# A graph layer's gather: one tile in five chunks fetched row by row by SyncE

## The chip, the cores and the metric

The kernel runs on one core of a Trainium2 chip. The metric is the device time of one execution in microseconds. A core has five engines with an instruction stream each: TensorE multiplies matrices (a weight load, then a matmul [...]), VectorE works element by element, ScalarE applies functions and copies, GpSimd is programmable and here only issues indirect gathers, and SyncE computes nothing and issues plain transfers. Transfers are carried out by 16 DMA engines [...]. Engines wait for each other and for transfers through semaphores.

## What is computed

Two relational graph layers on 50,000 nodes of 128 floats with 850,000 edges, then a residual layer norm. Cut to what matters:

```python
W   = einsum('rb,bio->rio', w_comp, basis)          # 16 relations from 8 bases
seg = dst * 16 + rel
agg = segment_sum(h[src], seg, 50000 * 16)          # sum the source rows by (target, relation)
msg = einsum('nri,rio->no', agg.reshape(N, 16, -1), W)
h   = relu(msg + h @ loop_w + bias)                 # twice: x -> H1 -> h
out = layernorm(x + h)
```

Edges come sorted by target node. The costly part is `h[src]`: 850,000 rows of 512 bytes, at random places in HBM, once for each layer.

## The kernel before

**Tiles and chunks.** 128 consecutive edges are a tile (6,641 tiles), ten tiles are a chunk (`K` = 10, so `C` = 665 chunks; the last one is short). Since the edges are sorted, the targets of a tile are few: a window of `WN` = 12 nodes from the tile's base node on. A chunk's tiles fall into one window of 128 nodes that starts at the chunk's base, `base_i[c]`.

**Preparation** (lines 151 to 293) loads the edges, turns them so that each tile's 128 source indices stand in one column of `src` and its slot numbers (relation and place in the window) in one column of `key`, computes the bases, and checks that all edges fit their windows (`good`). If they do, `chunked` runs (line 316), otherwise a slow general path, `summed`, which this input doesn't take.

**One chunk of one layer** (lines 379 to 419):

- `at(c)` loads the chunk's base node into a register of SyncE. SyncE loads the window's own 128 rows, `hw`, for the self loop, and in layer 2 also `xw` for the residual.
- Ten gathers (line 390, the helper is line 296): GpSimd issues one indirect transfer for each tile, 128 rows of 512 bytes, into `g[:, k, :]`. `g` has six buffers, so GpSimd may run up to six chunks ahead of TensorE.
- VectorE writes `hot` (line 392), a one-hot matrix of 192 slots (16 relations x 12 nodes) for every edge.
- TensorE multiplies each tile's rows by its one-hot matrix into `pa` (line 403), two tiles to a bank, three banks; ScalarE copies the bank to `aT` (line 410).
- After the second pair of tiles comes `finish` for the chunk before (line 415): `slots` sums over the relations (16 products with `W`, line 335); `nodes_of` moves the slots to nodes (`own`, line 347) and adds what the chunk before left over (`kept`, `shift`, line 351); the self loop is a transpose of `hw` (line 141), a copy to `hT` by ScalarE (line 143) and a product with `LOOP` (line 355); `ended` applies the relu and stores the window to `H1` from `h`, or in layer 2 adds the residual, normalises (`normed`: `st`, `mv`, `sd`, `rs`, `nm`, `o`) and stores to `out`. SyncE issues both stores.

**The order.** Each engine works through its instructions in order. The order is not that of the source: the framework's scheduler places instructions by its own costs, for instance the transpose of `hw` and two matmuls of the next tiles between the products with `W` and those with `own`, and the weight sums of the second layer (`combine(1)`, line 130, on VectorE), which are written at the end of the first layer, among the first chunks. The framework also gives every transfer one of its own semaphores in turn and puts the waits in.

**The layers.** Layer 2 gathers from `H1`, so its first gather waits for layer 1's last store.

Of the kernel before, what the change touches and what calls it, by code (L numbers as in the profile page):

```python
# [23 lines left out]
F32 = mybir.dt.float32  # L27
I32 = mybir.dt.int32
BF16 = mybir.dt.bfloat16
U8 = mybir.dt.uint8  # L30
AF = mybir.ActivationFunctionType
OP = mybir.AluOpType
# [4 lines left out]
P = 128  # L37
# [3 lines left out]
K = P // WN  # L41
S = K * WN
G = P // K * K
BATCH = 8
EPS = 1e-5
BANK = 512

# [6 lines left out]
def tile_rgcn_resnorm(  # L54
# [15 lines left out]
    nc = tc.nc  # L70
    N, D = x.shape
# [3 lines left out]
    C = -(-n_tiles // K)  # L75
# [6 lines left out]
    H1 = dram.tile([N, D], F32, name="H1")  # L82

    consts = ctx.enter_context(tc.tile_pool(name="consts", bufs=1))
# [16 lines left out]
    eps = consts.tile([P, 1], F32, name="eps")  # L101
    nc.vector.memset(eps, EPS)

# [42 lines left out]
    def column(j, first, ap):  # L146

        return bass.AP(tensor=edges.tensor, offset=edges.offset + j * E + first, ap=ap)
# [3 lines left out]
    src = consts.tile([P, n_groups * G], I32, name="src")  # L152
    key = consts.tile([P, n_groups * G], F32, name="key")

    base_i = consts.tile([1, C], I32, name="base_i")
    dist = consts.tile([P, C], F32, name="dist")
    slot = consts.tile([P, C], F32, name="slot")
    good = consts.tile([1, 1], I32, name="good")
    with tc.tile_pool(name="meta1", bufs=1) as m1, tc.tile_pool(name="meta", bufs=2) as mp:
# [14 lines left out]
        base1 = m1.tile([1, C], F32, name="base1")  # L174
        nc.vector.tensor_scalar(base1, tile_base[0:1], float(N - P), None, op0=OP.min)
        nc.vector.memset(base1[:, 0:1], 0.0)
        nc.vector.memset(base1[:, C - 1 :], float(N - P))
        nc.vector.tensor_copy(base_i, base1)

        spread = m1.tile([K, S], F32, name="spread")  # L180
        nc.gpsimd.iota(
# [12 lines left out]
        for c0 in range(0, C, D):  # L194
            cs = slice(c0, min(c0 + D, C))
            k = cs.stop - c0
# [7 lines left out]
            )  # L204
        nc.vector.memset(dist[:, C - 1 :], 0.0)
        nc.vector.tensor_tensor(dist[:, : C - 1], base[:, 1:], base[:, : C - 1], op=OP.subtract)
        n_batches = -(-n_groups // BATCH)
        picked = m1.tile([P, n_batches + 2], F32, name="picked")
        nc.vector.memset(picked, 0.0)
# [7 lines left out]
            op0=OP.is_le,  # L217
# [10 lines left out]
            op0=OP.is_lt,  # L228
# [3 lines left out]
        for i in range(n_batches):  # L232
            g0 = i * BATCH
            q = min(BATCH, n_groups - g0)
            t0 = g0 * G
# [7 lines left out]
            if whole < q:  # L243
# [29 lines left out]
                op0=OP.is_lt,  # L273
# [8 lines left out]
            for of, to, engine in ((srcf, src, nc.scalar.copy), (rel0, key, nc.vector.tensor_copy)):  # L282
                for h0 in range(0, q, BANK // P):
                    h = min(BANK // P, q - h0)
# [15 lines left out]
    def normed(t, m, sb):  # L300

        st = sb.tile([P, 6], F32, name="st")
        nc.vector.bn_stats(st[:m], t)
        mv = sb.tile([P, 2], F32, name="mv")
        nc.vector.bn_aggr(mv[:m], st[:m])
        sd = sb.tile([P, 1], F32, name="sd")
        nc.scalar.activation(sd[:m], mv[:m, 1:2], AF.Sqrt, bias=eps[:m])
        rs = sb.tile([P, 1], F32, name="rs")
        nc.vector.reciprocal(rs[:m], sd[:m])
        nm = sb.tile([P, 1], F32, name="nm")  # L310
        nc.vector.scalar_tensor_tensor(nm[:m], mv[:m, 0:1], -1.0, rs[:m], op0=OP.mult, op1=OP.mult)
        o = sb.tile([P, D], F32, name="o")
        nc.scalar.activation(o[:m], t, AF.Identity, bias=nm[:m], scale=rs[:m])
        return o

    def chunked():
        combine(0)
        with tc.tile_pool(name="gp", bufs=6) as gp, tc.tile_pool(name="hp", bufs=2) as hp, tc.tile_pool(
            name="sb", bufs=3
        ) as sb:  # L320

            def at(c):
                return nc.values_load(
                    base_i[0:1, c : c + 1],
                    engines=[mybir.EngineType.SP],
                    min_val=0,
                    max_val=N - P,
                    skip_runtime_bounds_check_because="bases are clamped to N - P, and no node is below 0",
                )

            def slots(c, k, aT, n):

# [28 lines left out]
            def ended(n, a, n0, xw):  # L361
                if n == 0:
                    h = sb.tile([P, D], F32, name="h")
                    nc.scalar.activation(h, a, AF.Relu)
                    nc.sync.dma_start(H1[ds(n0, P), :], h)
                else:
                    t = sb.tile([P, D], F32, name="t")
                    nc.vector.scalar_tensor_tensor(t, a, 0.0, xw, op0=OP.max, op1=OP.add)
                    nc.sync.dma_start(out[ds(n0, P), :], normed(t, P, sb))

            for n, of in enumerate((x, H1)):
                kept, late = None, None

                def finish(kept, c, k, aT, hw, n0, xw):
                    kept, a = nodes_of(c, k, slots(c, k, aT, n), kept, hw, n)
                    ended(n, a, n0, xw)
                    return kept

                for c in range(C):
                    ks = min(K, n_tiles - c * K)  # L380
                    n0 = at(c)
                    hw = sb.tile([P, D], F32, name="hw")
                    nc.sync.dma_start(hw, of[ds(n0, P), :])
                    xw = None
                    if n:
                        xw = sb.tile([P, D], F32, name="xw")
                        nc.sync.dma_start(xw, x[ds(n0, P), :])
                    g = gp.tile([P, K, D], F32, name="g")
                    for k in range(ks):
                        gather(g[:, k, :], of, src[:, c * K + k : c * K + k + 1])  # L390
                    hot = hp.tile([P, K, NR * WN], F32, name="hot")
                    nc.vector.tensor_tensor(  # L392
                        hot[:, :ks],
                        grid[:, None, :].to_broadcast([P, ks, NR * WN]),
                        key[:, c * K : c * K + ks, None].to_broadcast([P, ks, NR * WN]),
                        op=OP.is_equal,
                    )
                    aT = hp.tile([P, NR, S], F32, name="aT")
                    for k in range(0, ks, 2):
                        m = min(2, ks - k)  # L400
                        pa = ps_a.tile([P, BANK], F32, name="pa")
                        for i in range(m):
                            nc.tensor.matmul(  # L403
                                pa[:, i * NR * WN : (i + 1) * NR * WN],
                                g[:, k + i, :],
                                hot[:, k + i, :],
                                start=True,
                                stop=True,
                            )
                        nc.scalar.copy(  # L410
                            aT[:, :, k * WN : (k + m) * WN].rearrange("p r (i w) -> p i r w", w=WN),
                            pa[:, : m * NR * WN].rearrange("p (i r w) -> p i r w", i=m, w=WN),
                        )
                        if k == 2 and late is not None:
                            kept = finish(kept, *late)
                            late = None
                    if late is not None:
                        kept = finish(kept, *late)
                    late = c, ks, aT, hw, n0, xw
                finish(kept, *late)  # L420
                if n == 0:
                    combine(1)

# [188 lines left out]
```

## Time and profile before

| | |
|---|---|
| timed executions | 22,033.58 us, median of 3 (22,026.26 to 22,033.65) |
| profiled execution | span 16,729.1 us |
| TensorE | busy 13,415.4 us (80%) |
| its weight loads | 11,315.1 us (68%) |
| VectorE | 5,048.0 us (30%) |
| ScalarE | 4,657.3 us (28%) |
| GpSimd | 12,558.5 us (75%), 13,290 instructions |
| granted TensorE clock | 0.890 |
| DMA | 67 GB/s on average; GpSimd's queue (q0) 425,024 packets, SyncE's (q1) 505,723 |

The first row is the metric; the others come from one profiled execution, whose span is shorter than the timed executions. The page doesn't tell why. In the page's slices of the span all engines' shares are even over both layers. A matmul's share overstates how hard TensorE works, since matmuls overlap and their ends are modelled. Issue time of SyncE and ScalarE is not counted as busy; it stands in the timeline under "SPq" and "ACTq".

### The profile page before, as it was taken

What the parts mean: (1) busy time and instruction counts of PE and PEld (TensorE: products, weight loads), DVE (VectorE), ACT (ScalarE), POOL (GpSimd) and SP (SyncE); (2) the same over time, 40 slices, a digit from 0 to 9 for tenths busy, and PEclk for the clock granted to TensorE, in tenths of its full rate; (3) what the DMA queues carried; (4) which work ended last, traced back from release to release, by engine and by line L of the source; (5) the groups of instructions that cost most, each with busy time, mean ns of one, the idle gap of its engine ahead of it and who ended that gap; (6) DMA issues with size and microseconds to landing.
All of it is one profiled execution on the core that took longest, in us unless ns stands there. A gap on an engine that the chain in (4) does not pass through costs nothing.

```text
span 16729.1 us, 222138 instructions
## 1 busy us (share of the span) xinstructions
PE 13415.4 (80%) x78570; PEld 11315.1 (68%) x78570; DVE 5048.0 (30%) x10325; ACT 4657.3 (28%) x12650; POOL 12558.5 (75%) x13290
## 2 busy tenths in 40 slices
PE   6888888878888888888888888888878888888787
PEld 5666666666666666666666666666666666666666
DVE  4222222222222222222233333333333333333333
ACT  2222222222222222222223222222222222222222
POOL 6777777777777777777777777777777777777777
PEclk9888888888888888888888889898888888888888
DMA  3222222222222222222222222222222222222222
GB/s 75 64 64 64 64 64 64 64 64 64 64 64 64 64 64 64 64 64 64 64 66 69 69 69 69 69 69 69 69 69 69 69 69 69 69 69 69 69 69 66
DMA packets 934787, 1115.38 MB, mean 67 GB/s; under 512 B 272843, under 2 KB 721179, under 8 KB 933691
## 3 DMA queue, kind: packets, MB, share of 16 engines
q0 software_dynamic: 425024, 871.30, 18.4%
q1 hardware_dynamic: 505723, 228.35, 4.9%
q8 instruction: 649, 10.63, 0.3%
q14 instruction: 447, 3.66, 0.1%
q10 hardware_dynamic: 2944, 1.44, 0.0%
HBM read 1012.86 MB, written 87.16 MB: 66 GB/s over the span
## 4 chain that ended last, share of the span: by engine, by line
POOL 41%; PE 26%; DMA 17%; issue 16%; DVE 0%; POOLq 0%; ACT 0%; SPq 0%; DVEq 0%; ACTq 0%
POOL g L296 41%; PE ps L335 16%; DMA g<-H,src 8%; DMA g<-in_x_dram,src 8%; PE pa L403 6%; PE pn L347 1%; PE pn L351 1%; PE po L355 1%; PE po L141 0%; DMA raw<-in_edges_dram 0%; DMA first_i<-in_edges_dram 0%; POOLq L296 0%; PE pa L287 0%; DVE rel L263 0%; DVE rel L277 0%
## 5 line engine op out<-in xcount | busy, mean ns | idle before, releaser
L403 PE MATMUL pa<-hot,g 128*128 128x192 f32 x26564 | 6758.5, 367 | 3246.0 <-DMA g<-in_x_dram,src 1430.2
L296 POOL DMA_INDIRECT g<-in_x_dram,src x6641 | 6291.7, 947 | 2109.0 <-issue 1782.5
L296 POOL DMA_INDIRECT g<-H,src x6641 | 6265.8, 944 | 2039.9 <-issue 1781.9
L403 PEld LDWEIGHTS pa<-hot,g 128*128 128x128 f32 x26564 | 4307.9, 199 | 5052.1 <-ACT aT L410 1885.8
L335 PEld LDWEIGHTS ps<-w,aT 128*120 128x120 f32 x42560 | 6078.3, 221 | 2.1 <-ACT aT L410 0.8
L335 PE MATMUL ps<-w,aT 128*120 128x128 f32 x42560 | 6021.0, 311 | 0.2
L410 ACT COPY aT<-pa 128x384 f32<-128x384 f32 x6642 | 3173.9, 478 | 6146.0 <-PE pa L403 6144.3
L350 DVE TENSOR_SCALAR shift<-apart,dist 128x128 f32<-128x128 f32 x1328 | 466.0, 351 | 10148.7 <-PE pn L351 10148.7
L392 DVE TENSOR_TENSOR hot<-grid,key 128x1920 f32<-128x1920 f32 x1330 | 2866.0, 2155 | 1244.1 <-PE pa L403 1233.9
L337 ACT COPY slots<-ps 120x128 f32<-120x128 f32 x1330 | 353.9, 266 | 4871.6 <-PE ps L335 4871.6
L347 PE MATMUL pn<-slots,own 120*128 120x128 f32 x2660 | 649.2, 326 | 0.4
L353 ACT COPY kept<-pn 128x128 f32<-128x128 f32 x1330 | 353.8, 266 | 841.1 <-PE pn L351 841.1
L347 PEld LDWEIGHTS pn<-slots,own 120*128 120x128 f32 x2660 | 395.5, 187 | 283.3 <-ACT slots L337 283.3
L355 PE MATMUL po<-loop,hT 128*128 128x128 f32 x2660 | 515.0, 275 | 0.4 <-ACT hT L143 0.4
L351 PE MATMUL pn<-kept,shift 128*128 128x128 f32 x2656 | 513.2, 274 | 0.0
L343 DVE TENSOR_SCALAR own<-grid,slot 120x128 f32<-120x128 f32 x1330 | 448.5, 337 | 0.0
L358 DVE TENSOR_TENSOR pn<-pn,s 128x128 f32<-128x128 f32 x1330 | 399.1, 300 | 150.7 <-ACT kept L353 9.3
L355 PEld LDWEIGHTS po<-loop,hT 128*128 128x128 f32 x2660 | 403.3, 192 | 0.7 <-ACT hT L143 0.7
L351 PEld LDWEIGHTS pn<-kept,shift 128*128 128x128 f32 x2656 | 402.8, 191 | 0.2
L357 DVE TENSOR_TENSOR s<-po,bias 128x128 f32<-128x128 f32 x1330 | 373.8, 281 | 17.9 <-PE po L355 17.8
L141 PE MATMUL po<-ident,hw 128*128 128x128 f32 x1330 | 363.0, 273 | 8.9 <-DMA hw<-H 4.7
L143 ACT COPY hT<-po 128x128 f32<-128x128 f32 x1330 | 360.7, 271 | 12.5 <-DVE w L130 8.4
(72 smaller groups left out, 1817.3 us busy)
## 6 DMA issues: line engine op xcount, KB each, us to landing
g<-in_x_dram,src POOLq DMA_INDIRECT x6641
g<-H,src POOLq DMA_INDIRECT x6641
hw<-in_x_dram SPq DMA_DIRECT2D x665, 64.0 KB
H<-h SPq DMA_DIRECT2D x665, 64.0 KB
hw<-H SPq DMA_DIRECT2D x665, 64.0 KB
xw<-in_x_dram SPq DMA_DIRECT2D x665, 64.0 KB
out_dram<-o SPq DMA_DIRECT2D x665, 64.0 KB
raw<-in_edges_dram SPq DMA_DIRECT2D x18, 480.0 KB
```

What stands on the lines that cost most here:

```text
L296: nc.gpsimd.indirect_dma_start(out=to, out_offset=None, in_=of, in_offset=bass.IndirectOffsetOnAxis(ap=idx, axis=0))
L335: nc.tensor.matmul(ps[: k * WN], aT[:, r, : k * WN], W[n][:, r, :], start=r == 0, stop=r == NR - 1)
L343: nc.vector.tensor_scalar(own[: k * WN], grid[: k * WN, :P], slot[: k * WN, c : c + 1], None, op0=OP.is_equal)
L347: nc.tensor.matmul(pn, own[: k * WN], st[: k * WN], start=True, stop=not c)
L350: nc.vector.tensor_scalar(shift, apart, dist[:, c - 1 : c], None, op0=OP.is_equal)
L351: nc.tensor.matmul(pn, shift, kept, start=False, stop=True)
L355: nc.tensor.matmul(po, turned(hw, P, sb), LOOP[n], start=True, stop=True)
L357: nc.vector.tensor_add(s, po, BIAS[n])
L358: nc.vector.tensor_add(pn, pn, s)
L392: nc.vector.tensor_tensor(hot[:, :ks], grid[:, None, :].to_broadcast([P, ks, NR * WN]), key[:, c * K : c * K + ks, None].to_broadcast([P, ...
L403: nc.tensor.matmul(pa[:, i * NR * WN : (i + 1) * NR * WN], g[:, k + i, :], hot[:, k + i, :], start=True, stop=True,)
L410: nc.scalar.copy(aT[:, :, k * WN : (k + m) * WN].rearrange("p r (i w) -> p i r w", w=WN), pa[:, : m * NR * WN].rearrange("p (i r w) -> p i ...
```

## The change

The tenth tile of every fifth chunk (chunks 6, 11, 16 and on, 132 in all, in both layers) is no longer gathered by GpSimd. Instead SyncE fetches its 128 rows one by one with plain transfers of 512 bytes, whose addresses it loads, 16 at a time, from a table `where` in SBUF. The table holds the source indices of those tiles times 512, so bytes, made once from the edges. The rows land in one of three buffers of their own (`alone`) with a semaphore each (`landed`), and the matmul that reads the tile waits for all of them. A fetch stands in the program six chunks ahead of its use. To leave SyncE free, the loads and stores of the nodes' windows go to ScalarE, which loads eight bases at a time, also in bytes; a chunk's store is issued at the end of the next chunk. The whole is under `manual_schedule`: instructions stay in the order in which they are written. What it is for: to take gathers from GpSimd and give them to an engine that has time left.

```diff
+EVERY = 5
+ALONE = 3
+ATONCE = 16
+BASES = 8
...
+    by_rows = range(EVERY + 1, C - 1, EVERY)
+    where = consts.tile([P, max(1, -(-len(by_rows) // P)), P], I32, name="where")
...
-        nc.vector.tensor_copy(base_i, base1)
+        nc.vector.tensor_scalar(base_i, base1, float(D * 4), None, op0=OP.mult)
...
+        for j0 in range(0, len(by_rows), P):
+            m = min(P, len(by_rows) - j0)
+            w = m1.tile([P, P], I32, name="w")
+            t = by_rows[j0] * K + K - 1
+            nc.scalar.dma_start(w[:m], column(0, t * P, [[EVERY * K * P, m], [1, P]]))
+            nc.vector.tensor_scalar(where[:m, j0 // P, :], w[:m], float(D * 4), None, op0=OP.mult)
...
-        ) as sb:
+        ) as sb, tc.manual_schedule():
+
+            alone = [consts.tile([P, D], F32, name=f"alone{i}") for i in range(ALONE)]
+            landed = [tc.alloc_semaphore(f"landed{i}") for i in range(ALONE)]
...
             def at(c):
-                return nc.values_load(
-                    base_i[0:1, c : c + 1],
-                    engines=[mybir.EngineType.SP],
+                return nc.values_load_multi_w_load_instructions(
+                    base_i[0:1, c : min(c + BASES, C)],
+                    engines=[mybir.EngineType.Activation],
...
+            def fetched(of, j):
+
+                by, p, i = j // P, j % P, j % ALONE
+                used[i] += 1
+                count, name = used[i], f"rows{i}_{used[i]}"
+                for e0 in range(0, P, ATONCE):
+                    _, rows = nc.values_load_multi_w_load_instructions(
+                        where[p : p + 1, by, e0 : e0 + ATONCE],
+                        engines=[mybir.EngineType.SP],
...
+                    for e, row in enumerate(rows):
+                        one = nc.sync.dma_start(
+                            alone[i].bitcast(U8)[e0 + e : e0 + e + 1, :], flat(of)[ds(row, D * 4)][None, :]
+                        )
+                        one.then_inc(landed[i], 16)
+                        tc.no_tile_sem_insts.add(one.ins.name)
+                        tc.add_to_no_dep_group(name, one.ins)
+
+                def reads(inst):
+                    inst.wait_op(landed[i], 16 * P * count, "sem-ge")
+                    tc.declare_no_dep(inst.ins, group=name, reason="waits for all of the buffer's rows itself")
+                    tc.declare_fence(inst.ins, group=name)
+
+                return alone[i], reads
...
-                    nc.sync.dma_start(H1[ds(n0, P), :], h)
+                    return lambda: nc.scalar.dma_start(window(H1, n0), h.bitcast(U8))
...
-                    nc.sync.dma_start(out[ds(n0, P), :], normed(t, P, sb))
+                    o = normed(t, P, sb)
+                    return lambda: nc.scalar.dma_start(window(out, n0), o.bitcast(U8))
...
-                    n0 = at(c)
+                    if c % BASES == 0:
+                        bases = at(c)
+                    n0 = bases[c % BASES]
                     hw = sb.tile([P, D], F32, name="hw")
-                    nc.sync.dma_start(hw, of[ds(n0, P), :])
+                    nc.scalar.dma_start(hw.bitcast(U8), window(of, n0))
...
-                    for k in range(ks):
+                    if c + EVERY + 1 in by_rows:
+                        fetch[c + EVERY + 1] = fetched(of, by_rows.index(c + EVERY + 1))
+                    rows, reads = [g[:, k, :] for k in range(ks)], None
+                    for k in range(ks - (c in fetch)):
                         gather(g[:, k, :], of, src[:, c * K + k : c * K + k + 1])
...
+                    if c in fetch:
+                        rows[-1], reads = fetch.pop(c)
...
-                            nc.tensor.matmul(
+                            made = nc.tensor.matmul(
                                 pa[:, i * NR * WN : (i + 1) * NR * WN],
-                                g[:, k + i, :],
+                                rows[k + i],
...
+                            if reads is not None and k + i == K - 1:
+                                reads(made)
...
                     if late is not None:
-                        kept = finish(kept, *late)
+                        kept, store = finish(kept, *late)
+                    if store is not None:
+                        store()
```

## The prediction

> **What bounds the kernel now.** I read the page's chain that ended last, then the costliest groups, then who waited for whom, then stretches of the timeline in order of time.
>
> ```profile
> POOL 41%; PE 26%; DMA 17%; issue 16%; DVE 0%; POOLq 0%; ACT 0%; SPq 0%; DVEq 0%; ACTq 0%
> ...
> L403 PE MATMUL pa<-hot,g 128*128 128x192 f32 x26564 | 6758.5, 367 | 3246.0 <-DMA g<-in_x_dram,src 1430.2
> L296 POOL DMA_INDIRECT g<-in_x_dram,src x6641 | 6291.7, 947 | 2109.0 <-issue 1782.5
> L296 POOL DMA_INDIRECT g<-H,src x6641 | 6265.8, 944 | 2039.9 <-issue 1781.9
> ```
>
> The chain names GpSimd's gathers (41%), the issue time between them (16%) and, through the gathers' landings (17%), TensorE: it walks from a matmul to the gather that fed it and back along GpSimd. The two L296 rows are the bound: 947 ns and 944 ns each, and the idle time ahead of them, 2109.0 and 2039.9 us over 6,641 gathers each, is some 0.31 us a time and mostly put down to "issue", that is, to nothing that the profile shows. TensorE's L403 row waits 1430.2 us for gathered rows. So TensorE waits for GpSimd, not GpSimd for it; the timeline shows the beat:
>
> ```profile
> 6001.03 0.94 POOL L296 DMA_INDIRECT g<-in_x_dram,src  x1 [0.30 <-issue]
> 6002.28 0.94 POOL L296 DMA_INDIRECT g<-in_x_dram,src  x1 [0.30 <-issue]
> ```
>
> The starts are 1.25 us apart: I take 1.247 (0.944 + 0.303). 13,282 gathers x 1.247 = 16,563 of 16,729 us; the rest is 87 us ahead of the first gather, some 25 us lost beside the weight sums, 16 us between the layers and the tail. A chunk of ten gathers takes 12.47 us. TensorE is busy 13,415.4 / 1,330 = 10.09 us of it, ScalarE 3.50, VectorE 3.80.
>
> **A gap that the profile doesn't explain.** The timed median is 22,033.6 us, 5,304 above the profiled span: 1.317 times. No view says whether that is an amount added once or a slower beat. At a slower beat a gather is worth 1.247 x 1.317 = 1.642 us and five chunks give the other engines some 81 us; as an amount added once, a gather is worth 1.247 us and five chunks take 62. I take the slower beat, since the profiled execution's own time (16,730.9) equals its span, so that no fixed part outside the span shows there.
>
> [...] GpSimd's time to initiate is the bound, while the 16 DMA engines are some 2 tenths busy in the page's slices; [...] gathers beside the weight sums of line 130 do take 3.77 us in place of 0.94.
>
> **The change, part by part.**
>
> Gathers removed. The chunks 6, 11, 16 and so on below 664 are 132; each loses its tenth gather, in both layers: 264 x 1.247 = 329 us of the profiled span, 264 x 1.642 = 434 us at the timed beat. GpSimd has 49 gathers in five chunks: 61.1 us (80.5).
>
> Rows added to SyncE: 264 x 128 = 33,792 transfers of 512 B, which must fit, 128 of them, into those 61.1 us: 0.477 us a row (0.629 at the timed beat). This term decides. The trace of before bounds it:
>
> ```profile
> 8418.00 0.35 SPq L383 DMA_DIRECT2D hw<-H  x1
> 8418.56 0.35 SPq L387 DMA_DIRECT2D xw<-in_x_dram  x1
> ...
> 8419.42 0.33 SPq L383 DMA_DIRECT2D hw<-H  x1
> ```
>
> ```profile
> 71.33 0.26 SPq L256 DMA_DIRECT2D raw<-in_edges_dram  x1
> 71.69 0.28 SPq L252 DMA_DIRECT2D raw<-in_edges_dram  x1
> ```
>
> A transfer with an address from a register takes 0.33 to 0.35 us of SyncE for 128 partitions; one of a single partition at a fixed address 0.26 (L256). A row lies between: 0.30. From hw's end (8418.35) to xw's start are 0.21 us, with address arithmetic but no load; from xw's end (8418.91) to the next hw 0.51, with one load: so a load of one word costs about 0.30. The edges' addresses are multiplied by 512 once, ahead, so a row needs no arithmetic, and fixed addresses show gaps of 0.04 to 0.10 (71.59 to 71.69): I take 0.06. Sixteen words in one load cost at least a single one, 0.30 / 16 = 0.02 a row, and at most sixteen single ones, 0.30 a row[...]. Ends: 0.26 + 0.04 + 0.02 = 0.32 and 0.35 + 0.21 + 0.30 = 0.86 us a row[...]. I take 0.45[...]: 58 us for a tile, under 61.1, well under 80.5. SyncE has nothing else queued, and with three buffers it may run ten chunks ahead, so only its rate counts, not its latency. Hidden by GpSimd's 49 gathers.
>
> Landing wait. The matmul of the tenth tile waits for 128 rows; behind it on TensorE stand the chunk's last copy to aT and the next chunk. If SyncE keeps its rate the rows landed chunks ago: 0 us.
>
> Loads and stores of nodes moved to ScalarE: per chunk two (layer 1) or three issues of 0.33 to 0.36 plus gaps of 0.05 to 0.2[...]: 0.8 to 1.8 us on top of 3.50 of 12.2. Behind them on ScalarE stands the copy of pa, which frees TensorE's bank; three banks of two tiles cover some 3 us of TensorE. Hidden by the gathers.
>
> Order as written. Before, TensorE's transpose of hw and two L403 matmuls stand between the L335 sums and L347, so that the copies to slots and hT run beside them. As written, L347 waits the 0.36 us from the sums' end at 6002.60 to 6002.96, and the product with LOOP about 0.5 us after its transpose: 0.86 us a chunk, TensorE 10.09 + 0.86 = 10.95 of 12.2 us. In layer 2 ScalarE also waits in order for VectorE's chain s, pn, t, st, mv ahead of sd and o, some 2.9 us, and hot follows behind: I allow TensorE 1.2 us more, 12.1, just under 12.2. Hidden by the gathers, narrowly if the beat is the profile's.
>
> The second layer's weight sums (32 us of VectorE, beside which gathers take 3.77) move from layer 1's start to the layers' boundary: eight slow gathers x 2.8 = 23 us lost in either place, some of it now inside the 16 us of waiting for H. TensorE starts layer 2 some 32 us late, under the six chunks that g buffers hold. Net 0. Two loads and scalings of where: under 5 us, put at 0.
>
> Sum: 22,033.6 - 434 = 21,600 us.
>
> **Rivals.**
>
> A fixed gap: the same mechanism, 22,033.6 - 329 = 21,704. For it: no view shows a slower beat.
>
> SyncE becomes the bound. [...] For it: single loads cost 0.30 us, and the profile's beat leaves only 0.477 us a row. Against: at the timed beat it fits up to 0.629.
>
> TensorE becomes the bound through the written order. At 13.0 us a chunk in layer 2 alone: 665 x 0.53 = 352 us lost, 165 saved in layer 1: 22,220, slower. For it: 12.1 against 12.2 us in my own sum. Against: before, TensorE waits 3,246 us ahead of L403, 2.4 us a chunk, so it has that to give.
>
> Both effects cancel: 22,030, no change.
>
> **How the numbers follow.** Forecast at the slower beat 0.45; fixed gap 0.23; cancelled 0.06; TensorE bound 0.10; SyncE bound 0.16. Faster 0.68, same 0.06, slower 0.26. The likeliest gives 21,600. The range leaves out SyncE's case: from 21,540 (a few more us saved at the boundary) to 22,700 (TensorE's 13.0 grown to 13.7 in layer 2, as unknown).
>
> **What would show it.** Right: 6,509 gathers a layer at unchanged 0.944 + 0.303 us, SyncE issuing rows under 0.477 us apart, no wait of L403's tenth tile on the rows' buffers, a profiled span near 16,233 + 166 = 16,400. Wrong: rows 0.5 us apart or more and L403 waiting for them while GpSimd waits for g buffers; or GpSimd waiting for TensorE, with TensorE waiting on slots and hT.

## The result, and the profile after

The changed kernel takes 26,526.18 us (median of 4, 26,519.24 to 26,529.12), the kernel before beside it 22,029.92 us: **1.204 times**, 95% interval 1.2021 to 1.2063. The change makes the kernel 20% slower.

One fact is needed to read every number below: on one chip, met in two groups of runs, the kernel before takes 16,730 us (**chip A**), on three others 21,317 to 21,335 us (**chips B**; the comparison above, at 22,030, is 3% longer still and is counted with them), and so each run is compared only with the kernel before on its own chip. The profile of before that the prediction rests on shows 16,729 us, so it shows the first group; the times of before that it was to forecast are of the second.

The page of the changed kernel, from its parts on busy time, the clock, the chain that ended last and the costliest groups:

```profile
PE 13937.4 (53%) x78570; PEld 12884.4 (49%) x78570; DVE 5063.1 (19%) x10327; ACT 4646.6 (18%) x12650; POOL 12335.7 (47%) x13026
...
another core or an unknown queue 49%; PE 26%; ACT 11%; issue 7%; DVE 4%; ACTq 2%; DMA 1%; POOL 0%; DVEq 0%; SPq 0%; POOLq 0%
...
L312 POOL DMA_INDIRECT g<-H,src x6509 | 6156.8, 946 | 7217.7 <-PE pa L465 5312.2
L312 POOL DMA_INDIRECT g<-in_x_dram,src x6509 | 6178.0, 949 | 6891.2 <-PE pa L465 4992.6
L465 PE MATMUL pa<-hot,g 128*128 128x192 f32 x26036 | 6481.0, 416 | 1064.9 <-ACT aT L474 910.2
L401 PE MATMUL pn<-slots,own 120*128 120x128 f32 x2660 | 1017.2, 484 | 10696.5 <-ACT slots L391 9849.2
```

GpSimd is gone from the chain (0%, before 41%). A gather still takes 946 to 949 ns; what grew is the idle time ahead of the gathers, 14,109 us in both layers against 4,149, and most of it now ends with TensorE's L465, that is, with the release of a `g` buffer: GpSimd waits for TensorE. TensorE hardly waits for gathered rows any more (one wait of 36.4 us at L465, before 1,430 us at L403 for layer 1's rows). It waits at L401, the product with `own`, for ScalarE's copy `slots`: 9,849 us. And half of the chain is put down to an unknown releaser. The waits say where that sits:

```profile
ACT slots L391 <- remote: 14050.5, 1311, 66.8
POOL g L312 <- PE pa L465: 10304.9, 1307, 25.2
...
PE pn L401 <- ACT slots L391: 9849.2, 1118, 66.6
```

"Remote" means that no instruction in the trace ended at a moment that explains the wait. One chunk of the timeline shows what that hides (some lines of TensorE's matmuls, of ScalarE, and the first and last of ten gathers with the first of the next ten):

```profile
8002.49 0.95 POOL L312 DMA_INDIRECT g<-in_x_dram,src  x1 [8.85 <-PE pa L465]
...
8003.27 0.86 ACT L474 COPY aT<-pa 128x384 f32<-128x384 f32 x2 [0.54 <-PE pa L465]
8003.36 3.66 PE L389 MATMUL ps<-w,aT 128*120 128x128 f32 x32
...
8013.75 0.95 POOL L312 DMA_INDIRECT g<-in_x_dram,src  x1 [0.30 <-issue]
8016.77 0.27 ACT L391 COPY slots<-ps 120x128 f32<-120x128 f32 x1 [12.63 <-remote]
...
8017.08 0.79 PE L401 MATMUL pn<-slots,own 120*128 120x128 f32 x2 [10.07 <-ACT slots L391]
...
8023.10 0.95 POOL L312 DMA_INDIRECT g<-in_x_dram,src  x1 [8.40 <-PE pa L465]
```

The 16 weight sums end at 8007.02 by the records. ScalarE has nothing else to do from 8004.13 on, and still its copy of their result starts at 8016.77, **9.75 us later**. The semaphore that the copy waits for is TensorE's, and the trace has its steps as events: the step comes at 8016.74, 0.03 us ahead of the copy. So ScalarE starts at once, and what is late is the step of TensorE's semaphore, the **release** of the sums. Behind the copy stands L401, behind L401 the rest of TensorE's stream, behind that the release of `g`, and GpSimd, done with its ten gathers at 8014.7, stands still until 8023.10. The two engines take turns: 12.2 us of gathers, 2.1 us to the copy, 6.3 us to the next gather, 20.6 us in all, where the forecast had a chunk's gathers hide TensorE's work. In 1,034 of the 1,330 chunks the copy comes like this, behind ten gathers in a row, in eight of ten of these 2.1 to 2.3 us after the end of the last. I call the time from the end of the last sum to the start of `slots` the **lateness**. Its mean over the 1,330 chunks is the main number of what follows. The matmuls' ends are modelled, so a lateness can be a release that is held or sums that ended later than the model has it; this profile doesn't part the two, one further down does. On chip A the same model is right within 0.04 us.

### The profile page after: what moved, and what is told of

Read it like the earlier page. It is cut to its first block, busy times and chain, and to the rows that moved or that the text cites. A ratio compares the mean times of both kernels' runs of the same rounds, so it can differ in the third digit from the quotient of the medians.

```text
span 26527.3 us, 282445 instructions
## 1 busy us (share of the span) xinstructions
PE 13937.4 (53%) x78570; PEld 12884.4 (49%) x78570; DVE 5063.1 (19%) x10327; ACT 4646.6 (18%) x12650; POOL 12335.7 (47%) x13026
## 4 chain that ended last, share of the span: by engine, by line
another core or an unknown queue 49%; PE 26%; ACT 11%; issue 7%; DVE 4%; ACTq 2%; DMA 1%; POOL 0%; DVEq 0%; SPq 0%; POOLq 0%
PE pa L465 14%; ACT aT L474 6%; PE po L409 4%; PE pn L401 4%; PE ps L389 3%; PE pn L405 2%; ACTq L440 1%; ACT kept L407 1%; ACT slots L391 1%; ACT hT L150 1%; ACT o L329 1%; DVE pn L412 1%; DVE st L319 1%; DVE s L411 1%
## 5 line engine op out<-in xcount | busy, mean ns | idle before, releaser
L465 PE MATMUL pa<-hot,g 128*128 128x192 f32 x26036 | 6481.0, 416 | 1064.9 <-ACT aT L474 910.2
L465 PEld LDWEIGHTS pa<-hot,g 128*128 128x128 f32 x26036 | 6061.8, 260 | 1334.9 <-ACT aT L474 1163.8
L401 PE MATMUL pn<-slots,own 120*128 120x128 f32 x2660 | 1017.2, 484 | 10696.5 <-ACT slots L391 9849.2
L401 PEld LDWEIGHTS pn<-slots,own 120*128 120x128 f32 x2660 | 638.9, 299 | 10957.1 <-ACT slots L391 10068.4
L389 PE MATMUL ps<-w,aT 128*120 128x128 f32 x42560 | 4904.1, 274 | 5.3 <-issue 4.9
L389 PEld LDWEIGHTS ps<-w,aT 128*120 128x120 f32 x42560 | 4862.8, 184 | 7.5 <-issue 5.1
L409 PE MATMUL po<-loop,hT 128*128 128x128 f32 x2660 | 1053.7, 498 | 759.6 <-ACT hT L150 567.1
L409 PEld LDWEIGHTS po<-loop,hT 128*128 128x128 f32 x2660 | 664.1, 311 | 1271.8 <-ACT hT L150 1045.0
L405 PE MATMUL pn<-kept,shift 128*128 128x128 f32 x2656 | 810.5, 407 | 0.0
L405 PEld LDWEIGHTS pn<-kept,shift 128*128 128x128 f32 x2656 | 694.5, 319 | 0.2
```

What stands on the lines that cost most here:

```text
L389: nc.tensor.matmul(ps[: k * WN], aT[:, r, : k * WN], W[n][:, r, :], start=r == 0, stop=r == NR - 1)
L401: nc.tensor.matmul(pn, own[: k * WN], st[: k * WN], start=True, stop=not c)
L405: nc.tensor.matmul(pn, shift, kept, start=False, stop=True)
L409: nc.tensor.matmul(po, turned(hw, P, sb), LOOP[n], start=True, stop=True)
L465: made = nc.tensor.matmul(pa[:, i * NR * WN : (i + 1) * NR * WN], rows[k + i], hot[:, k + i, :], start=True, stop=True,)
```

## The experiments

Means over each profile, worked out from the trace: the lateness of `slots`, and the granted TensorE clock from the results.

| kernel | chip A: us (ratio) | lateness, clock | chips B: us (ratio) | lateness, clock |
|---|---|---|---|---|
| before | 16,730.6 | 0.04, 0.89 | 21,320.6; 21,334.9; 21,316.9 | 3.6, 0.80 |
| changed | not met | | 26,026.8 (1.221); 26,039.1 (1.221); 26,036.8 (1.222) | 7.5; 7.4; 7.4, 0.76 (7.7 and 0.75 in the profile above) |
| written order alone | 17,052.9 (one run, 1.019) | 0.04, 0.90 | 22,854.9 (1.073) | 3.0, 0.78 |
| changed, no rows | 17,053.5 (one run, 1.019) | 0.04, 0.90 | 22,505.9 (1.055) | 3.1, 0.79 |
| changed, scheduler's order | 16,462.5 (one run, 0.984) | 0.09, 0.82 | 24,774.9 (1.163) | 6.7, 0.75 |
| the same, no rows | 16,731.6 (1.000) | 0.04, 0.89 | | |
| one block for the rows | 16,887.7 (1.009) | 0.04, 0.91 | | |
| every tenth chunk | 16,986.3 (1.015) | 0.04, 0.90 | | |
| sums apart | | | 22,017.3 (1.032) | 2.5, 0.78 |
| sums spread | | | 21,843.0 (1.024) | 0.8, 0.78 |
| half the sums | | | 22,996.3 (1.079) | 3.8, 0.71 |

### The change taken apart, on chip A

The kernel before once more, then three kernels beside it. In the diffs below "-" is the changed kernel's line; the order alone starts from the kernel before.

> The kernel before, unchanged, profiled once more: its timed executions (22,030 us) and the profiled one shown so far (16,729 us) differ, and the kernel after takes 26,520 in both. Order theory (TensorE's release of the 16 sums comes late and the written order has nothing to put in the gap): the longer executions of before show late releases as well, some 4 us a chunk of lateness that its order hides only in part; a profile at 22,030 would show ScalarE's slots copy late after the sums. Row theory (SyncE's 33,792 transfers alone hold the release up): no lateness without rows, so a profile at 22,030 has its extra 4 us a chunk elsewhere, in GpSimd's gathers.

It took 16,764.2 us, and 16,727.9 as the median of the runs beside the other three: on this chip the gap between the profile of before and its times isn't there at all.

```diff
-        ) as sb:
+        ) as sb, tc.manual_schedule():
```

> Only the written order is kept, on the kernel before: all 13,282 gathers on GpSimd, nodes' loads and stores on SyncE, no rows. Order theory: TensorE waits 2.5 us or more behind the sums in each chunk and the time is over 22,500 us, up to 26,000. Row theory: the sums are released at once (0.04 us), the time stays between 16,700 and 22,100 us.

17,052.9 us, 1.9% above before. The waits of this kernel (the second column is how often):

```profile
ACT slots L337 <- PE ps L335: 5038.7, 1330, 5.6
POOL g L296 <- issue: 3764.6, 12288, 2.7
ACT aT L410 <- PE pa L403: 3733.5, 3041, 50.2
...
PE pa L403 <- ACT aT L410: 2135.6, 1212, 2.7
ACT sd L307 <- DVE mv L305: 1451.1, 665, 2.3
```

Here all 1,330 waits of `slots` end with the sums themselves and none is remote. The loss is in layer 2: from its `slots` to the next a chunk takes 12.90 us there on average against 12.46 before, and 12.47 in layer 1. ScalarE waits in order for VectorE ahead of `sd` (1,451 us, 122 before), and TensorE's matmuls wait for `aT` behind it (2,136 us, 344 before).

```diff
-    by_rows = range(EVERY + 1, C - 1, EVERY)
+    by_rows = range(0)
```

> The kernel after with all tiles gathered by GpSimd: no rows on SyncE, order as written, nodes' loads and stores on ScalarE. Order theory: the chunk stays near 20 us, 25,000 us or more. Row theory: the release comes within 2.6 us of the sums' end as it does in the chunks of the kernel after in which SyncE stands still; a chunk takes 13 to 14 us and the whole 17,500 to 18,500 us.

17,053.5 us, the same as the order alone: loads and stores from ScalarE cost nothing here.

```diff
-        ) as sb, tc.manual_schedule():
+        ) as sb:
```

> The kernel after without the written order: the framework's scheduler places the instructions, rows on SyncE and nodes on ScalarE stay. Order theory: other matmuls stand between the sums and the product with own, TensorE's wait there goes, and the time falls to 22,100 us or less. Row theory: SyncE still delays the release by some 9 us in each chunk and the time stays over 25,000 us.

With the rows and the scheduler's order, 16,462.5 us: 265 us **below** before. The gathers' groups and SyncE's own lines of this kernel (durations in ns, least, median, most):

```profile
L312 POOL DMA_INDIRECT g<-in_x_dram,src x6509 | 6183.7, 950 | 2079.4 <-issue 1865.3
L312 POOL DMA_INDIRECT g<-H,src x6509 | 6157.3, 946 | 2009.9 <-issue 1850.2
```

```profile
L371 SPq DMA_DIRECT2D alone<-in_x_dram x16896: 224/225/363, 94.3 to 8130.6; - x199
```

```profile
L363 SPq TENSOR_LOAD <-where x2112: 998/1257/1527, 93.2 to 16290.4; - x192
```

GpSimd is the bound again, with idle time only of the kind that it always had, and 132 gathers fewer a layer. A row is 0.225 us of issue; with its register move and the gaps the rows start 0.318 us apart, and a load of 16 addresses adds 1.26 / 16 = 0.08: 0.40 us a row, measured as the mean distance without longer waits. So on chip A rows on SyncE are as cheap as the forecast needed.

### The same parts on a chip B

> The kernel after, unchanged, beside the kernel before on the chip of this comparison. In the last runs before took 16,728 us here and in the first result 22,030. Order theory: the written order costs what order alone showed, 324 us, and the rows give back up to 329: ratio 0.99 to 1.01 where before takes 16,728, with TensorE waiting behind the sums; 1.20 only where before takes 22,030. Row theory: the ratio is about 1.20 on every chip, since the delay comes with the rows.

> Rows and nodes on ScalarE, scheduler's order, now timed. Order theory: ratio 0.984 to before where before takes 16,728 us (16,462 in the one look), and below 1.0 also where before takes 22,030, since the scheduler's order covers late releases. Row theory: above 1.1 where before takes 22,030.

> The written order alone, timed. Order theory: ratio 1.019 where before takes 16,728 us (17,053 in the one look); 1.05 to 1.20 where before takes 22,030. Row theory: 1.02 in both.

> Written order and nodes on ScalarE without rows, timed. Order theory: as order alone in both conditions, 1.019 or 1.05 to 1.20, so that ScalarE's loads and stores cost nothing. Row theory: 1.02 in both.

The edits are those above. All four lie together on one chip, beside the kernel before at 21,320.6: the changed kernel 26,026.8, with the scheduler's order 24,774.9, the order alone 22,854.9, no rows 22,505.9. Adding the rows to the kernel without rows costs 3,521 us, 16%, and this edit alone takes the lateness from 3.1 to 7.5 us. Written order and moved loads cost 1,185. The scheduler's order saves only 1,252 of the whole, since the lateness is 6.7 us there too. The group of ScalarE's copy without rows, then with them and the scheduler's order:

```profile
L391 ACT COPY slots<-ps 120x128 f32<-120x128 f32 x1330 | 352.6, 265 | 8436.0 <-remote 7650.0
```

```profile
L391 ACT COPY slots<-ps 120x128 f32<-120x128 f32 x1330 | 353.9, 266 | 12602.5 <-remote 11212.5
```

Mostly "remote" in both, and larger with the rows. So the rows make the late release later: shown by the edit in the written order, and in the scheduler's order in line with the kernel before, its nearest partner (3.6 us). How they do it is not shown.

They don't do it alone. In the scheduler's order, 319 of the 1,330 bursts of sums have no gather beside them (none from 2.5 us ahead of the first sum to the end of the last), and in 303 of these SyncE issues rows all the same: their copies are 0.12 us late on average and 0.98 at most, while the 999 with gathers and rows are 8.8 us late. In the changed kernel (second profile in the table) 272 bursts have gathers but no row, 2.6 us late, 1,046 have both, 8.7 us late, and the 12 with no gather 0.04. So on chips B the release is late beside gathers, and rows lengthen that; without gathers rows do hardly anything to it. These are stretches sorted within two profiles; no run took the gathers away.

### Number, size and dose of the transfers, on chip A

> The kernel before, unchanged, beside its own timed executions, for a profile in the condition in which it takes over 21,000 us. Theory of the late release (TensorE's release of the 16 sums comes late, by some 3 us beside gathers alone and by 7 to 10 beside rows): slots starts 2 to 4 us after the sums' end in the mean, not 0.04, and the chunk takes 16 us in place of 12.5. Rival (GpSimd's gathers are slower there): slots 0.04 us after the sums, gathers 1.6 us apart.

> The kernel after without rows and without the written order: what is left is nodes' loads and stores on ScalarE. Theory of the late release: no rows, no exposed order, so ratio to before 0.98 to 1.00 (order alone took 22,855 us and the same with ScalarE's loads 22,506, 1.5% less). Rival (ScalarE's loads delay its copies): over 1.01.

```diff
-                for e0 in range(0, P, ATONCE):
...
+                one = nc.sync.dma_start(
+                    alone[i].bitcast(U8), flat(of)[0 : P * D * 4].rearrange("(p d) -> p d", p=P)
+                )
...
```

> The kernel after with each of the 264 fetched tiles brought by one transfer of the first 128 rows of the nodes in place of 128 transfers of single rows, and no register loads for them: other rows than the edges name, so it leaves the fetch of the right rows out. Order, buffers, semaphores and the number of gathers stay. Theory of the late release by SyncE's transfers: the time falls to that without rows less 2%, ratio 1.03 to 1.06 to before where before takes 21,300 us. Rival (the tile's own buffer and wait, or the uneven gathers, cost the time): ratio stays at 1.2.

```diff
-EVERY = 5
+EVERY = 10
```

> The kernel after with one tile in ten chunks fetched row by row: half as many rows, 16,896 in all. Theory of the late release: SyncE is busy in half of the time, and the ratio lies midway between 1.055 (no rows) and 1.22, at 1.12 to 1.16. Rival (a fixed cost of having rows at all): 1.2 or more.

These four came to chip A: before 16,730.5; without rows and with the scheduler's order 16,731.6 (1.0001, 0.9992 to 1.0009), so that ScalarE's loads and stores cost nothing; one block 16,887.7 (1.0094, 1.0077 to 1.0111); every tenth chunk 16,986.3 (1.0153, 1.0136 to 1.0170). No release was late in any (0.04 us in each), so they say nothing on the rows' part in it. They do price the written order: the block kernel, free of 264 gathers and of all rows, is still 157 us above before. It saves 150 us in layer 1 (last gather at 8,253.6 in place of 8,404.2) and gives back some 320 in layer 2 and the tail. The changed kernel itself never met chip A. From the block kernel and the order alone I estimate it there between 16,890 and 17,050 us; that is not measured.

### Where the late release is exposed, on a chip B

> The changed kernel once more, beside the kernel before. Theory (what the change costs depends on whether TensorE's releases of the weight sums reach ScalarE late): where the kernel before takes about 16,730 us the releases are on time, the written order costs about 0.32 us a chunk and the rows give little back, so 16,890 to 16,950 us, ratio 1.01, and slots starts within 0.1 us of the last sum; where before takes 21,300 or more, 1.20 to 1.22 and slots 7 to 8 us late. Rival (the rows themselves or the written order cost the same everywhere): 1.20 in either case.

> The kernel before, one look for its profile. Where it takes 21,300 us or more, theory: its copies to slots start 2 to 6 us after the last sum, as in the kernel with the order alone (3.0), but the two products of the next tiles, which the scheduler put between, cover a part. Rival (a slower beat of GpSimd's gathers): slots within 0.1 us of the last sum, and gathers 1.6 us apart. Where it takes 16,730 us both expect 0.04 us and 1.25 us.

The kernel before in a profile of a chip B (one execution, 21,369.9 us): its chain that ended last, its gathers, and its waits.

```profile
PE 57%; another core or an unknown queue 20%; issue 17%; ACT 4%; DVE 2%; DMA 0%; POOL 0%; SPq 0%; DVEq 0%; ACTq 0%; POOLq 0%
...
L296 POOL DMA_INDIRECT g<-H,src x6641 | 6264.5, 943 | 4711.6 <-PE pa L403 2454.5
...
L296 POOL DMA_INDIRECT g<-in_x_dram,src x6641 | 6288.5, 947 | 4044.4 <-issue 1697.1
```

```profile
ACT slots L337 <- remote: 7926.7, 1122, 68.1
...
POOL g L296 <- PE pa L403: 3878.8, 870, 13.6
POOL g L296 <- issue: 3463.4, 11349, 0.6
...
POOL g L296 <- remote: 1077.0, 443, 9.3
```

The gathers take 943 and 947 ns and stand 3,463.4 / 11,349 = 0.305 us apart, exactly as on chip A: there is **no slower beat**. GpSimd waits 3,879 us for TensorE and 1,077 for the unknown, 4,956 together, which is about the 4,638 us between its two spans. The kernel before has late releases of its own, 3.6 us on average, and on a chip B its bound is TensorE with these late releases, not GpSimd.

```diff
...
-                        if k == 2 and late is not None:
-                            kept, store = finish(kept, *late)
-                            late = None
+                        if k == 0 and late is not None and ks == K:
+                            early = slots(late[0], late[1], late[2], n)
+                        if k == 8 and late is not None:
+                            kept, store = finish(kept, *late, early)
+                            late = None
```

> The changed kernel with the 16 weight sums of the chunk before written after its first pair of tiles, and what uses their copy (own, shift, the self loop, the end) after the last pair, so that eight products lie between. Theory of the exposed late release: TensorE has some 5 us of work in that gap, so where slots comes 7 to 8 us late the wait ahead of own falls from about 11 to 5 us a chunk or less and the ratio from 1.20 to 1.00 to 1.10; where releases are on time, the 0.86 us ahead of own are gone too and the time is below 16,730 us, 16,400 to 16,700. Rival (the late release is one face of a slower TensorE or slower rows, and moves with the wait): stays within 2% of the changed kernel in either case.

22,017.3 us: moving L401 from directly behind the sums to eight products later takes the ratio from 1.221 to **1.032** (1.0298 to 1.0338), with all rows still there. The product's group, and GpSimd's waits:

```profile
L401 PE MATMUL pn<-slots,own 120*128 120x128 f32 x2660 | 622.4, 322 | 1.4 <-ACT slots L391 1.4
```

```profile
POOL g L312 <- PE pn L401: 3022.9, 668, 8.9
POOL g L312 <- PE pa L467: 2817.4, 634, 23.1
```

The wait at L401, 9,602 us in the changed kernel on this chip, is 1.4 us. GpSimd still waits for TensorE, but for 5,840 us in place of 9,684.

This profile also parts the two readings of a lateness, since TensorE has work behind the sums:

```profile
8001.81 5.32 PE L389 MATMUL ps<-w,aT 128*120 128x128 f32 x32
...
8006.97 2.12 PE L467 MATMUL pa<-hot,g 128*128 128x192 f32 x12
...
8008.24 0.94 POOL L312 DMA_INDIRECT g<-in_x_dram,src  x1 [0.30 <-issue]
8011.37 0.27 ACT L391 COPY slots<-ps 120x128 f32<-120x128 f32 x1 [8.88 <-remote]
```

The last sum ends at 8007.13 by the records and six products of tiles (two matmuls each) by 8009.09, 0.325 us apart. The sums and the six products owe seven steps of TensorE's semaphore, and seven steps come, from 8011.34 to 8011.60, each 0.043 us after the one before. Products don't end that close to each other by the records (0.325 us apart), and in every profile of chip A the steps of TensorE are 0.109 us apart or more. So I read it that TensorE had gone on multiplying and its **steps were held**, then passed on in a row, 2.2 us after the last gather's end. There are 1,134 such rows of three steps or more in this profile, and nine in ten begin 2.0 to 2.3 us after the end of the gather before them. Every profile of a chip B has steps under 0.06 us apart, 303 to 6,319 of them. So on chips B steps of TensorE are held while gathers run, where its matmuls go on by the records; what holds them the trace doesn't say.

```diff
-                for r in range(NR):
+                for r in range(NR) if part is None else range(4 * part, 4 * part + 4):
...
+                        if k < 8 and late is not None and ks == K:
+                            early = slots(late[0], late[1], late[2], n, k // 2, None if k == 0 else early)
...
```

> As the kernel with the sums apart, and the 16 sums themselves written four at a time after the first four pairs of tiles, so that no burst of 16 short products stands ahead of the copy to slots; own follows one pair later. Theory A (a release is late because it follows a burst of 32 short instructions of TensorE): slots starts within 1 us of the last sum even where the changed kernel's comes 7 to 8 us late, and the ratio is 0.97 to 1.05 there. Theory B (any release of TensorE is late while SyncE issues rows): slots still comes 5 us or more late, own waits for it, ratio 1.12 or more. Where releases are on time both give 16,400 to 16,700 us.

21,843.0 us (1.0237, 1.0217 to 1.0256), lateness 0.8 us. By the measure that was named, the copy to `slots`, the first theory is the nearer. But the hold has only moved: now the copy of `aT` from the second pair of tiles, behind the first four sums, starts 2.9 us after its products' modelled end on average, with ScalarE free (0.1 us in the changed kernel on this chip). So a release can be late without a burst of sixteen sums, and the first theory isn't shown. Why is the kernel no faster than before? Its chain that ended last names a new bound:

```profile
SPq 57%; issue 34%; PE 6%; ACT 1%; another core or an unknown queue 0%; DMA 0%; DVE 0%; POOL 0%; ACTq 0%; DVEq 0%
```

and TensorE now waits for rows, which it hardly did in the kernel with the sums apart (second line):

```profile
PE pa L470 <- DMA alone<-in_x_dram: 524.0, 112, 8.2
```

```profile
PE pa L467 <- DMA alone<-H: 247.9, 102, 4.2
```

I took the distances between the starts of all 33,792 rows from the trace. Here SyncE pauses for a buffer at 1 tile of 264 (in the changed kernel at 255, for 6,870 us in all), so it works without a break, and the rows are 0.641 us apart, with the sums apart 0.636: 33,792 x 0.641 = 21,661 us of the span of 21,867. With TensorE's wait moved away, SyncE is what this kernel runs into; with the sums apart it is near that (25% of the chain, TensorE 33%). On chip A the same instructions are 0.401 us apart, and the median distance, 0.32 us, is the same on both; on chips B a quarter of the rows are 0.71 us and more behind the one before. Here too gathers make the difference: in the changed kernel on this chip rows that start during a gather or within 0.5 us of its end are 0.67 us apart, those without a gather for 2.5 us 0.40, as on chip A.

```diff
-                for r in range(NR):
-                    nc.tensor.matmul(ps[: k * WN], aT[:, r, : k * WN], W[n][:, r, :], start=r == 0, stop=r == NR - 1)
+                for r in range(0, NR, 2):
+                    nc.tensor.matmul(ps[: k * WN], aT[:, r, : k * WN], W[n][:, r, :], start=r == 0, stop=r == NR - 2)
```

> The changed kernel with 8 weight sums a chunk in place of 16: every second relation is left out of the computation. Where the kernel before takes 21,300 us or more, theory (TensorE's load itself brings on the halved clock and the late releases): the granted clock rises from 0.76 to over 0.85, slots starts less than 2 us after the last sum, and the time falls by far more than the 1.83 us a chunk that the sums take in the records: 16,400 to 19,200 us, ratio 0.77 to 0.90. Rival (the release is late for a reason outside TensorE, such as the rows or the semaphores): still 7 us late, and only the eight sums' 1.83 us x 1,330 = 2,434 us are saved: 23,600 us, ratio 1.10. Where before takes 16,730 us: TensorE's chain in the written order falls from 13.3 to 11.4 us a chunk, below GpSimd's 12.2, so 16,400 to 16,500 us, ratio 0.98 to 0.99.

> The changed kernel in the same call, as the partner of the kernel with half the sums. Where before takes 16,730 us, which no run of the changed kernel has met yet: 16,890 to 16,950 us, ratio 1.01, as with one block transfer in place of the rows (1.009) and below the order alone (1.019). Where before takes 21,300 us or more: 1.22 as before. Rival (rows or order cost the same everywhere): 1.2 in both.

Half the sums: 22,996.3 us (1.0787), beside 26,036.8. The theory behind this run fell: the granted clock went **down**, from 0.760 to 0.711, and the time is far from 19,200. The rival wasn't met either: the lateness halved, 7.4 to 3.8 us, and 3,040 us were saved in place of 2,434. So with fewer sums their release is less late, and the halved clock is not what makes it late.

## Why the prediction was wrong, step by step

**What bounds the kernel.** Right for the execution that was profiled, wrong for the ones that were timed. On chips B GpSimd is at 0% of the chain of before.

**The gap.** This step failed first. The prediction saw 22,034 against 16,729 and chose "a slower beat", 1.642 us a gather, over an amount added once. It was neither: the beat is 1.25 us in every profile here, and the time goes into TensorE's late releases, chunk by chunk. GpSimd is not the bound on chips B, so the 434 us were not to be had in the way in which the prediction counted them, as beats of GpSimd; what fewer gathers alone are worth there, no run shows.

**Gathers removed, rows added.** On chip A both terms hold. Predicted was a span near 16,400 us (13,018 gathers x 1.247 us, and 166 at the ends) with SyncE at 0.45 us a row inside 0.477; with the scheduler's order the span is 16,460.1 at 0.40 us a row. The load of 16 addresses, put between 0.02 and 0.30 us an address, is 0.08; the 0.45 was my estimate between the ends 0.32 and 0.86. On chips B the row's price is another: 0.56 us in the changed kernel and 0.64 where TensorE waits less, so 82 us a tile against the 80.5 that the prediction had to give. In the changed kernel this isn't what binds (SyncE waits for free buffers 6,870 us), but in the kernel with the sums spread it is. The rival "SyncE becomes the bound" so comes true in that one, on a chip B alone, at 21,843 us.

**"So only its rate counts."** This step failed next, and the term that it put at nothing was the largest. The rows cost TensorE's releases: from 3.1 to 7.5 us of lateness, and 3,521 us, on one chip and in one edit. No view of before could show it, since that profile has no late release at all; the one warning was its span, 24% below the times.

**Landing wait and loads on ScalarE.** Right. Among the waits of the changed kernel is none of TensorE for `alone`. The changed kernel without rows equals the order alone on chip A, and with the scheduler's order it equals before (1.0001). On chips B moving loads and stores to ScalarE even saves 1.5% (22,505.9 against 22,854.9).

**Order as written.** Mis-sized on chip A, and wrong in kind on chips B. TensorE at 12.1 us a chunk in layer 2, "hidden narrowly", was 12.90 in the order alone, so it shows; the rival with TensorE as the bound put it at 13.0 and a net loss of 187 us, and the block kernel's 157 is close to that. On chips B the step "L347 waits the 0.36 us from the sums' end" becomes a wait of 7 to 10 us for the copy to `slots`: the scheduler had put two products there, the written order puts none. The prediction's own sign of being wrong, GpSimd waiting for TensorE and TensorE for `slots`, is what came, but not for its reason, an order that costs a little too much. Moving the wait away brings back most of the loss, 4,022 of 4,704 us.

**The weight sums of layer 2.** Right: from the last gather of layer 1 to the first of layer 2 are 15.6 to 16.3 us before and 17.3 with the order alone on chip A.

**The half clock.** I first took the halved clock on chips B for a cause. In the profile of the changed kernel above the granted clock is either whole or half; of its 1,328 stretches of half clock all but the last are 3.413 us long or a multiple of it, 972 of them 10.24 us. Parts of that profile in order of time show which comes first (columns: stretch, its length, busy us of TensorE, its weight loads, VectorE, ScalarE and GpSimd, then the clock, DMA share, GB/s):

```profile
8003.00:8007.00 4.00, 4.00 (x36) 3.81 (x34) 0.00 (x0) 0.86 (x2) 3.09 (x4) 1.00 0.29 83
8008.00:8011.00 3.00, 0.00 (x0) 0.00 (x0) 0.00 (x0) 0.00 (x0) 2.33 (x3) 1.00 0.21 57
8012.00:8017.00 5.00, 0.00 (x0) 0.00 (x0) 0.00 (x0) 0.23 (x1) 2.09 (x3) 0.50 0.15 40
8017.00:8021.00 4.00, 3.56 (x12) 3.16 (x13) 1.19 (x3) 0.80 (x5) 0.00 (x0) 0.50 0.00 1
```

TensorE is idle from 8007 while its clock is still whole; the half clock comes at 8011.75, 4.7 us after the last sum, and is still there beside the first products after the wait. So it is in most places: when the half clock begins, TensorE has been idle for over 1 us in 1,193 of the 1,328 stretches, for 3.35 us at the median. In this kernel the half clock follows the wait and doesn't begin it. What brings it on is not shown: in the profile of before on chip A 746 of 757 stretches begin with TensorE idle for less than 1 us. What it costs no run prices (L401's matmuls take 484 ns, L347's in the profile of before 326). The kernel with half the sums gives TensorE less to do, 57,290 matmuls in place of 78,570, and its granted clock is the lower one, 0.711 against 0.760.

**What stays open.** What holds the steps of TensorE's semaphore beside gathers on three chips and not on a fourth, whether it is the gathers' issue or their transfers, why rows from SyncE lengthen it, why it is shorter behind half the sums, and whether the slower rows, which come beside gathers too, have the same cause. What differs between the chips is not known. In the changed kernel the lateness falls on the copy that follows the sums (ScalarE's copies of `aT` start on average 0.1 us later than products and ScalarE allow), and it is 0.04 us in the last chunks, after all gathers have ended.

The scheduler's order with the rows beats the kernel before on chip A (0.984, one run) and loses 16% on a chip B; no kernel here beat the one before on both.

## What to carry to other kernels

When a profile's span is a quarter below the timed median, as here (16,729 us against 22,034), it isn't a profile of what was timed: don't scale its durations, get a profile of an execution that takes the long time, and ask which engine is the bound there. In an order written by hand, put independent work of the same engine between a burst and the first instruction that needs its result by way of another engine; here eight products in that place were worth 15% of the time. And work given to an "idle" engine is to be priced by what it does to the others' releases too (here 4.4 us of lateness and 3,521 us), not by its rate alone. Where a wait is "remote", see when the semaphore itself steps, and what else runs until then: here that, and not the modelled ends, told a held release from a slow engine.

## What the hardware showed that was not expected

- The same kernel takes 16,730 us on one chip and some 21,320 on three others, 27% more, with gathers of 943 to 947 ns, 1.25 us from one to the next, on both.
- On chips B, a step of TensorE's semaphore can come 9.7 us after the modelled end of the last of 32 short matmuls, while the same burst's step takes 0.04 us on chip A. The steps are held beside gathers and then come in a row, 0.043 us apart, mostly 2.0 to 2.3 us after the end of a gather.
- Single-row transfers from SyncE, 0.32 us apart at the median, come 0.40 us apart on average on one chip and 0.56 to 0.64 on others, with the issue's own median unchanged at 0.225 us. In the changed kernel on one of these chips it is 0.67 beside gathers and 0.40 without.
